# Two outlook-attention layers: layer 1's weights reach their source row in the table transfer, not in 0/1 matmuls

## The chip, the cores and the metric

The kernel runs on one core of one Trainium2 chip, in float32. The metric is the device time of one launch in microseconds (us). Three runs of the kernel before took 3530.87, 3531.84 and 3535.32 us; the median is 3531.84 us. The profile is one further execution, which took 3516.74 us.

## The reference, cut to what matters

The input is 8 images of 56 x 56 pixels with 384 channels. Two layers follow each other, each a group normalisation, a convolution-like attention and a residual. Layer 1 is:

```python
a = jax.nn.softmax((x @ W_attn + b_attn).reshape(B, H * W, heads, k * k), axis=-1)   # heads 6, k 3
v = x @ W_v + b_v
vp = jnp.pad(v, ((0, 0), (1, 1), (1, 1), (0, 0)))
patches = stack([vp[:, i:i + H, j:j + W] for i in range(k) for j in range(k)])
y = einsum('bpKhd,bphK->bphd', patches, a)          # nine weighted neighbours per pixel and head
return y @ W_proj + b_proj
```

Each pixel weighs its 3 x 3 neighbours. Seen from a neighbour (the source), its weight belongs to a pixel one row above, on the same row, or one row below. The kernel wants the weights ordered by source row, so each weight with row offset `ki` has to move by `ki - 1` rows; weights whose source lies outside the image must not count. Layer 0 is of the same kind with nine softmaxes per head and a fold.

## The kernel before, in words

**Tiling.** Two images are laid over each other (`R = 112` rows) and one image column of both is one step. Columns are taken in patches of `PX = 7`; a patch of an image pair is a *group*, numbered g, and there are `NG = 32` groups. Layer 1's main loop (`for step in range((NG + 1) * PX)`, L1016) runs seven steps m = 0 to 6 per group. In layer 1 nearly every operation goes through a wrapper that keeps the order in which the code is written (`InOrder`, L124; its instructions all show as L132, matmuls as L119, transposes as L122). So the order on each engine is the order of the loop. Layer 0's vector and scalar operations are ordered by the framework's scheduler.

**What a step does.** `attend` (L843) multiplies 128 normalised tokens by the joint weights for logits and values (tile `bank`), and VectorE adds the biases into `lgt` and `v`. When the column number is a multiple of 8, `attend` does nothing. GpSimd's queue writes `v` to the value table `vtab1` (`spread`, L311).

**What a group does, in the steps that follow its own.** `keep_logits` (L867) writes the logits to DRAM at m = 0 (`lgtab`), `read_logits` (L879) reads them back with image rows on the partitions (tile `at`, m = 1), `weigh` (L893, m = 3) and `share` (L901, m = 4) make the softmax on VectorE with one exp on ScalarE, and `move` (L909, m = 5) does this:

- three matmuls with the constant 0/1 matrices `shift` (L168), one per row offset `ki`, give `pw` in PSUM, the weights of source row r. Out-of-image weights are zeroed by the matrices. TensorE carries each as two instructions.
- nine ScalarE copies bring `pw` into `wz`, each 112 x 42, so that the seven pixels of the patch lie one element apart in neighbouring slots (the band).
- one transfer from ScalarE's queue writes `wz` to a weight table in DRAM (`ztab1`, three of them in turn): 112 rows x 9 slots, one piece of 3 x 42 floats (504 bytes) each.

At m = 0 of the next group `fetch` (L938) issues from SyncE's queue, in this order: four reads of the table as band matrices (`z`), two reads of the values (`vp`), then, at m = 1, the load of the residual (`x1t`, `load`, L797) and the read of the logits (`at`). From m = 3 on, the contraction `pc`, the output projection `po` and the transposes `pt` of that group are taken from a list of jobs (`Jobs`, L339), two per step.

**The tables' zeros.** What no transfer of weights writes is zeroed once, in layer 0: `clear_weights` (L215) issues four transfers from SyncE for each of the three tables of layer 0 (steps 5, 14, 21) and of layer 1 (steps 35, 42, 49). `inside` (L182) holds for each row offset and row a 1, or a 0 where the neighbour is outside.

**Instructions per engine around the change.** At m = 5, ScalarE's order is: two copies `yT<-pc`, the nine `wz` copies, the table transfer, `ot` (a transposed output), two copies `yT<-pc`, the normalisation `xn` of the next patch. TensorE's order is: 48 `pc` matmuls, the six `pw` instructions, `bank`, a transpose, 36 `pc`, `bank`, a transpose, and then `po`, which needs every `yT`.

Of the kernel before, what the change touches and what calls it, by code (L numbers as in the profile page):

```python
# [8 lines left out]
F32 = mybir.dt.float32  # L9
AF = mybir.ActivationFunctionType  # L10
# [5 lines left out]
def two_outlook_layers(  # L16
# [38 lines left out]
    R = IMG * H  # L55
    MARGIN = 2
# [8 lines left out]
    PX = 7  # L65
# [4 lines left out]
    HEADS0, HEADS1 = 12, 6  # L70
    D0, D1 = C // HEADS0, C // HEADS1
    K, K2 = 3, 9
# [12 lines left out]
    PY1, NPY1, SX1, SY1 = 8, 7, PX + 2, 10  # L85
    ROW1 = HEADS1 * PX
# [8 lines left out]
    EP1, FIRST1 = 11, 4  # L95
    SLOT0, SLOT1 = EP0 * ROW0, EP1 * ROW1
    LINE0, LINE1 = SX0 * SLOT0 + ROW0, SX1 * SLOT1 + ROW1
# [20 lines left out]
    def matmul(*args, **kwargs):  # L118
        tc.keep_in_program_order(nc.tensor.matmul(*args, **kwargs))  # L119
# [48 lines left out]
    shift = const.tile([R, K, R], F32, name="shift")  # L168
    gpsimd.memset(shift, 0.0)
    for k in range(-1, 2):  # L170
        s = shift[:, k + 1, :]
# [10 lines left out]
    inside = const.tile([R, K, PH_ALL], F32, name="inside")  # L182
# [12 lines left out]
    def fill(table, first, dims, width):  # L195

        src = zeros[: dims[0][1], :width]
        if len(dims) > 1:
            src = src.unsqueeze(1).to_broadcast([dims[0][1], dims[1][1], width])
        tc.keep_in_program_order(  # L200
            nc.sync.dma_start(bass.AP(table.tensor, table.offset + first, [*dims, [1, width]]), src)
        )
# [12 lines left out]
    def clear_weights(table, line, part, sx, slot, row, first, e, ep):  # L215
        fill(table, 0, [[part, MARGIN * line // part]], part)
        fill(table, (MARGIN + R) * line, [[part, (MARGIN + 1) * line // part]], part)
        top = MARGIN * line
        fill(table, top, [[line, R]], first * row)
        fill(table, top + (first + e) * row, [[line, R], [slot, sx]], (ep - e) * row)  # L220

    def clears():

        yield 3, lambda: clear_v(vtab0, SX0, 2)

        yield 4, lambda: fill(
            ztab0[0], MARGIN * LINE0 + FIRST0 * ROW0, [[LINE0, R], [SLOT0, 2]], E0 * ROW0
        )
        for n, t in enumerate(ztab0):
            yield (5, 2 * PX, 3 * PX)[n], lambda t=t: clear_weights(  # L230
                t, LINE0, 366, SX0, SLOT0, ROW0, FIRST0, E0, EP0
            )
        yield 4 * PX, lambda: clear_v(vtab1, SX1, 1)
        for n, t in enumerate(ztab1):
            yield (5 + n) * PX, lambda t=t: clear_weights(
                t, LINE1, 350, SX1, SLOT1, ROW1, FIRST1, K, EP1
            )
# [116 lines left out]
    ps = ctx.enter_context(tc.tile_pool(name="ps", bufs=1, space=PS))  # L354
# [429 lines left out]
    def layer1(pools, base, last_of_layer0, late_w):  # L784
        vector, scalar, sync = (InOrder(e) for e in (nc.vector, nc.scalar, nc.sync))
# [53 lines left out]
        NW = SX1 * K * ROW1  # L839
# [68 lines left out]

        def move(g):  # L909

            at = lgs.pop(g)

            pw = ps.tile([R, K, PX, K, HEADS1], F32, tag="f", name=f"pw1_{g}")
            for ki in range(K):
                matmul(
                    pw[:, K - 1 - ki].rearrange("r x f h -> r x (f h)"),
                    shift[:, ki, :],
                    at.rearrange("r x (i j) h -> r x i (j h)", j=K)[:, :, ki, :],
                    start=True, stop=True,
                )  # L920

            wz = wzs[g % 2]
            step = K * ROW1 + 1
            for kj in range(K):
                dst = wz[:, kj * K * ROW1 : kj * K * ROW1 + PX * step].rearrange("r (m e) -> r m e", e=step)
                dst = dst[:, :, : K * ROW1].rearrange("r m (e h o) -> r e m h o", e=K, h=HEADS1)
                for e in range(K):
                    scalar.copy(dst[:, e, :, :, 0], pw[:, e, :, kj, :])
            table = ztab1[g % NTAB]
            scalar.dma_start(  # L930
                bass.AP(
                    table.tensor, table.offset + MARGIN * LINE1 + FIRST1 * ROW1,
                    [[LINE1, R], [SLOT1, SX1], [1, K * ROW1]],
                ),
                wz[:, :NW].rearrange("r (s e) -> r s e", s=SX1),
            )

        def fetch(g, due):  # L938
            pair, px = divmod(g, NPX)
# [76 lines left out]
        for step in range((NG + 1) * PX):  # L1016
            g, m = divmod(step, PX)
# [3 lines left out]
            read, first, second, moved = (0, 2, 3, 4) if last else (1, 3, 4, 5)  # L1021
# [10 lines left out]
            if g and m == moved:  # L1032
                move(done)
# [69 lines left out]
```

## Time and profile before

| | us |
|---|---|
| median of three runs (3530.87 to 3535.32) | 3531.84 |
| the profiled execution: its time / its span | 3516.74 / 3514.6 |
| TensorE busy in the span | 3427.7 (98%) |
| ScalarE, VectorE, GpSimd busy | 1173.3, 1935.8, 1202.1 |
| layer 1's `pw` matmuls: 192 instructions, mean 290 ns each | 29.7 in the instruction's own time |
| `wz` copies: 288, mean 269 ns | 31.8 |
| table writes `ztab<-wz`: 32 of 496.1 KB, issue to landing | 4.4 |

How to read it: the span runs from the first to the last instruction; the time of the execution has a little around it. Matmuls overlap each other in the array, so the sum of their own times is more than the time they take from the engine; the distance from start to start tells that. A transfer has two times: how long its issue holds the queue, and how long it takes from issue to landing. Layer 1 begins at about 2320 us; its groups follow each other from about 2390 to 3440 us.

### The profile page before, as it was taken

The numbers are of one execution on the slowest core, as the hardware profiler recorded it, in microseconds if no ns is written. First come the engines' busy times: TensorE is split into PE (matmuls) and PEld (weight loads), VectorE is DVE, ScalarE is ACT, GpSimd is POOL, SyncE is SP. The second block draws the span as 40 slices with busy tenths as digits, with TensorE's granted clock in tenths as the row PEclk, the third lists the DMA queues.
The fourth block names the chain that finished last, engine by engine and source line by source line (L and its number), as shares of the span: only waits on it lengthen the run. The fifth ranks groups of instructions, "written<-read, shape, count | busy, mean of one in ns | idle before, by whom it ended". The sixth has DMA issues, their size and how long they took to land. (4 is left out here: it accounts for less than half of the span.)

```text
span 3514.6 us, 72311 instructions
## 1 busy us (share of the span) xinstructions
PE 3427.7 (98%) x29014; PEld 2353.0 (67%) x29014; DVE 1935.8 (55%) x4680; ACT 1173.3 (33%) x2727; POOL 1202.1 (34%) x1833
## 2 busy tenths in 40 slices
PE   7899999999999999999999999988999999999998
PEld 5577777777777777777777777655666666666665
DVE  6666666667666676667766666633333333333331
ACT  4333223333333233333322223223434434343432
POOL 2543434434344344344443444331222222221220
PEclk8999999999999999999999999999999999999998
DMA  8999988688886878887757776676878787878775
GB/s 270 286 288 282 275 275 267 212 256 253 279 263 209 272 221 273 259 252 256 236 181 226 245 225 193 222 271 192 226 221 234 217 229 219 243 205 237 216 219 147
DMA packets 672893, 839.34 MB, mean 239 GB/s; under 512 B 302190, under 2 KB 566574, under 8 KB 668462
## 3 DMA queue, kind: packets, MB, share of 16 engines
q1 hardware_dynamic: 321422, 537.46, 47.9%
q10 hardware_dynamic: 323872, 210.54, 22.7%
q0 software_dynamic: 27264, 86.73, 7.5%
q8 instruction: 228, 3.74, 0.5%
q14 instruction: 107, 0.88, 0.1%
HBM read 512.95 MB, written 321.66 MB: 237 GB/s over the span
## 5 line engine op out<-in xcount | busy, mean ns | idle before, releaser
L119 PE MATMUL bank<-wa_t,xn 128*112 128x288 f32 x4032 | 1086.9, 409 | 11.4 <-ACT v L562 7.8
L574 POOL TENSOR_TENSOR at<-at,den 112x972 f32<-112x972 f32 x224 | 504.6, 2253 | 1193.1 <-DVE den L573 1137.8
L119 PEld LDWEIGHTS bank<-wa_t,xn 128*112 128x112 f32 x4032 | 693.4, 177 | 263.7 <-issue 34.3
L119 PE MATMUL po<-yT,wo_t 128*128 128x448 f32 (+1 forms) x2304 | 817.5, 494 | 5.3 <-DVE x1t L685 4.8
L119 PEld LDWEIGHTS po<-yT,wo_t 128*128 128x128 f32 x2304 | 432.8, 191 | 293.5 <-issue 185.4
L119 PE MATMUL pc<-z,vp 121*32 121x49 f32 (+1 forms) x17664 | 487.9, 254 | 25.3 <-DMA vp<-vtab 10.4
L119 PEld LDWEIGHTS pc<-z,vp 121*32 121x32 f32 (+1 forms) x17664 | 441.3, 131 | 103.3 <-issue 79.5
L550 DVE TENSOR_REDUCE mx<-bank 112x36 f32<-112x324 f32 x672 | 327.6, 487 | 310.6 <-PE bank L119 303.7
L317 POOL DMA_DIRECT2D vtab<-v x392 | 213.1, 547 | 825.3 <-DVE v L132 810.4
L119 PE MATMUL bank<-wc_t,xn 128*128 128x438 f32 x1176 | 478.8, 543 | 5.0 <-DMA wo_t<-in_wo 5.0
L119 PE MATMUL bank<-wv_t,xn 128*128 128x384 f32 x1176 | 417.9, 492 | 0.0
L555 ACT ACTIVATE at<-at 112x972 f32<-112x972 f32 x224 | 227.0, 1014 | 344.9 <-DVE at L551 317.6
L551 DVE TENSOR_TENSOR at<-bank,mx 112x324 f32<-112x324 f32 x672 | 328.8, 489 | 21.1 <-DVE mx L550 0.5
L119 PEld LDWEIGHTS bank<-wc_t,xn 128*128 128x128 f32 x1176 | 214.0, 191 | 174.8 <-issue 162.4
L119 PEld LDWEIGHTS bank<-wv_t,xn 128*128 128x128 f32 x1176 | 219.5, 190 | 139.6 <-issue 18.7
L619 ACT COPY wt<-pw 112x120 f32<-112x120 f32 x224 | 58.0, 259 | 654.0 <-PE pw L119 591.2
L597 POOL TENSOR_TENSOR pre<-at,at 112x108 f32<-112x108 f32 (+1 forms) x440 | 238.0, 541 | 110.4 <-DVE wt L620 96.0
L567 DVE TENSOR_TENSOR d<-at 112x432 f32<-112x432 f32 x224 | 141.7, 632 | 204.7 <-ACT at L555 204.7
L132 DVE TENSOR_TENSOR lgt<-bank,ba_t 128x54 f32<-128x54 f32 x196 | 41.7, 213 | 361.3 <-PE bank L119 361.3
L132 DVE SCALAR_TENSOR_TENSOR x1t<-po,bo_t,x1t 128x448 f32<-128x448 f32 (+1 forms) x156 | 97.7, 626 | 248.9 <-PE po L119 248.9
L664 ACT COPY yT<-pc 128x294 f32<-128x294 f32 x256 | 103.4, 407 | 368.9 <-PE pc L119 325.9
L535 ACT ACTIVATE xn<-xin,bias,scale 128x224 f32<-128x224 f32 x336 | 172.9, 566 | 67.2 <-PE bank L119 36.0
(100 smaller groups left out, 2924.6 us busy)
## 6 DMA issues: line engine op xcount, KB each, us to landing
z<-ztab SPq DMA_DIRECT2D x64, 2352.0 KB, 18.0
vp<-vtab SPq DMA_DIRECT2D x64, 1536.0 KB, 8.3
ztab<-wt ACTq DMA_DIRECT2D x336, 183.8 KB, 6.8
vp<-vtab SPq DMA_DIRECT2D x64, 945.0 KB, 12.0
xres<-xT SPq DMA_DIRECT2D x32, 1176.0 KB, 10.1
xin<-xT ACTq DMA_DIRECT2D x54, 672.0 KB, 7.3
z<-ztab SPq DMA_DIRECT2D x128, 258.4 KB, 4.5
x1t<-x SPq DMA_DIRECT2D x26, 1176.0 KB, 19.0
```

The lines of the kernel that those rows point to most:

```text
L119: tc.keep_in_program_order(nc.tensor.matmul(*args, **kwargs))
L132: return lambda *args, **kwargs: tc.keep_in_program_order(op(*args, **kwargs))
L317: queue.dma_start(bass.AP(table.tensor, table.offset + first, [[line, rows], [(R + GAP) * line - PX * C, n], [1, C]],), v.unsqueeze(1).to_ ...
L535: nc.scalar.activation(to[:, i, :, rows], xin[:, i, :, rows], AF.Identity, bias=bias[:, i, b : b + 1], scale=scale[:, i, b : b + 1],)
L550: nc.vector.tensor_reduce(mx[:, pi, :], pl.rearrange("r q a -> r a q"), AX.X, ALU.max)
L551: nc.vector.tensor_tensor(at[:, pi], pl, mx[:, pi, :].unsqueeze(1).to_broadcast([R, K2, PH]), ALU.subtract)
L555: nc.scalar.activation(at, at, AF.Exp, scale=SCALE0)
L567: nc.vector.tensor_add(d4, at[:, :, 0:4], at[:, :, 4:8])
L574: nc.gpsimd.tensor_tensor(at, at, den.unsqueeze(2).to_broadcast([R, K, K2, PH]), ALU.mult)
L597: nc.gpsimd.tensor_tensor(dst, terms[0], terms[1], ALU.add)
L619: nc.scalar.copy(mid[:, 0 : E0 : E0 - 1, :], pw[:, 0 : E0 : E0 - 1, :])
L664: nc.scalar.copy(yT[:, :, :, b, rows_of], pc.rearrange("p i n y m -> p i m (n y)"))
```

## The change

In layer 1 the weights stay on the partition of the pixel they belong to, and the transfer into the table writes them to the source's row. The nine copies become nine activations (`Copy` with a scale) that read the softmax result `at` in SBUF; the scale is the 0 or 1 of `inside` for the two outer row offsets, and the constant 1.0 for the middle one. The single transfer becomes three, one per row offset e, each to the row above, the same row, or the row below, with pieces of 42 floats (168 bytes). `clear_weights`, which layer 0 uses too, zeroes two more strips of each table: the places in the first and last row that no weight is moved to. The three matmuls and the PSUM tile `pw` of layer 1 are gone; layer 0 still uses `shift`.

```diff
@@ clear_weights @@
+        fill(table, top + first * row, [[slot, sx]], row)
+        fill(table, top + (R - 1) * line + (first + e - 1) * row, [[slot, sx]], row)
@@ move @@
-            pw = ps.tile([R, K, PX, K, HEADS1], F32, tag="f", name=f"pw1_{g}")
-            for ki in range(K):
-                matmul(
-                    pw[:, K - 1 - ki].rearrange("r x f h -> r x (f h)"),
-                    shift[:, ki, :],
-                    at.rearrange("r x (i j) h -> r x i (j h)", j=K)[:, :, ki, :],
-                    start=True, stop=True,
-                )
+            at = at.rearrange("r x (i j) h -> r i x j h", j=K)
...
-                for e in range(K):
-                    scalar.copy(dst[:, e, :, :, 0], pw[:, e, :, kj, :])
+                for ki in range(K):
+                    scalar.activation(
+                        dst[:, K - 1 - ki, :, :, 0], at[:, ki, :, kj, :], AF.Copy,
+                        scale=inside[:, ki, 0:1] if ki != 1 else 1.0,
+                    )
             table = ztab1[g % NTAB]
-            scalar.dma_start(
-                bass.AP(
-                    table.tensor, table.offset + MARGIN * LINE1 + FIRST1 * ROW1,
-                    [[LINE1, R], [SLOT1, SX1], [1, K * ROW1]],
-                ),
-                wz[:, :NW].rearrange("r (s e) -> r s e", s=SX1),
-            )
+            for e in range(K):
+                scalar.dma_start(
+                    bass.AP(
+                        table.tensor,
+                        table.offset + (MARGIN + 1 - e) * LINE1 + (FIRST1 + e) * ROW1,
+                        [[LINE1, R], [SLOT1, SX1], [1, ROW1]],
+                    ),
+                    wz[:, :NW].rearrange("r (s e w) -> r e s w", s=SX1, e=K)[:, e],
+                )
```

In the built programs the order on TensorE, VectorE and GpSimd in layer 1 is otherwise the same; ScalarE's differs by the lines above. In layer 0 the scheduler orders some operations of steps 5 to 12 differently.

## Prediction

> **What bounds the kernel now.** I read the page's first two parts for the whole, then the stage in which the change lies: one window over the steady groups of layer 1, two stretches of the timeline, the waits of SyncE's queue, and the DMA queues in short windows.
>
> ```profile
> PE 3427.7 (98%) x29014; PEld 2353.0 (67%) x29014; DVE 1935.8 (55%) x4680; ACT 1173.3 (33%) x2727; POOL 1202.1 (34%) x1833
> ...
> DMA  8999988688886878887757776676878787878775
> ```
>
> ```profile
> 2427.00:3397.00 970.00, 968.48 (x7496) 606.67 (x7495) 307.59 (x652) 389.83 (x1143) 216.37 (x399) 1.00 0.80 225
> ```
>
> The second fence is layer 1 from the table write of group 2 (2427.09) to that of group 30 (3397.11): TensorE is busy 968 of 970 us, so it sets the pace, 970.0 / 28 = 34.64 us per group. But the last columns say that the DMA engines are busy 80% of the same time. That calls for a second look: is there a chain of transfers that is nearly as long as the pace?
>
> ```profile
> 2911.77 0.31 ACTq L132 DMA_DIRECT2D ztab<-wz  x1
> ...
> 2916.18 1.79 SPq L132 DMA_DIRECT2D z<-ztab  x4
> ...
> 2918.26 0.86 SPq L132 DMA_DIRECT2D vp<-vtab  x2
> ...
> 2919.23 4.25 SPq L132 DMA_DIRECT2D x1t<-x  x1
> ...
> 2939.05 0.84 DVE L132 TENSOR_REDUCE mx<-at 112x42 f32<-112x378 f32 x1 [4.35 <-DMA at<-lgtab]
> ...
> 2942.39 0.55 DVE L132 TENSOR_TENSOR at<-at,den 112x378 f32<-112x378 f32 x1
> ...
> 2944.09 0.91 PE L119 MATMUL pw<-at,shift 112*112 112x126 f32 x6
> ...
> 2944.84 2.37 PE L119 MATMUL bank<-wc_t,xn 128*128 128x438 f32 x6
> 2945.03 0.99 ACT L132 COPY wz<-pw 112x42 f32<-112x42 f32 x9 [0.39 <-PE pw L119]
> 2946.06 0.31 ACTq L132 DMA_DIRECT2D ztab<-wz  x1
> ```
>
> ```profile
> SPq L132 <- DMA ztab<-wz: 546.1, 31, 25.4
> ```
>
> There is, and it is a **loop**. SyncE's queue holds the `z` reads until the table write has landed (31 waits); `vp`, `x1t` and the next logits (`at`) stand behind them in the same queue; VectorE's `mx` waits for `at`; the softmax ends in `at<-at,den`; then come `pw`, `wz` and the next table write. Over 28 groups the means from one write's issue are: `z` issued at 4.27, `mx` starts at 27.60, softmax done at 31.50, and 1.97 from the start of `pw` to the next issue: 33.47 us. TensorE's 34.64 is longer by only 1.2 us.
>
> ```profile
> q10 hardware_dynamic: 721, 0.36, 91.9%
> ...
> q1 hardware_dynamic: 2535, 3.76, 80.5%
> q0 software_dynamic: 373, 1.27, 19.3%
> q10 hardware_dynamic: 912, 0.19, 6.2%
> ...
> q1 hardware_dynamic: 675, 0.14, 95.9%
> ...
> q10 hardware_dynamic: 424, 0.09, 91.2%
> ```
>
> Queues in windows (packets, MB, share of 16 engines). The first line is the table write alone (2844.5 to 2846). The next three (2918 to 2936, from just behind the `z` issue to near the landing of `at`) add up to 106%: there the engines are full, so what starts later ends later by as much. The last two are small packets: the logits' read (2937.5 to 2938.2) and their write (3163.5 to 3164), 216 bytes each.
>
> **What the Trainium skill says.** "DMA: Bandwidth & Descriptors", section "Issuing engines are not separate DMA queues": transfers of all queues share the same 16 engines. The 106% agrees. Same page, "Why small descriptors are slow (HBM only)": each packet carries a fixed overhead beside its bytes, so a third of the bytes costs more than a third of the time. The trace agrees: 721 packets of 504 bytes took 1.5 us x 16 x 0.919 / 721 = 30.6 ns each; those of 216 bytes 0.7 x 16 x 0.959 / 675 = 15.9 (read) and 0.5 x 16 x 0.912 / 424 = 17.2 (write). "ScalarE: Activation LUTs", section "What ACT_TABLE_LOAD costs": an operand per partition, such as the new scale, adds about 93 ns to an ACTIVATE. No run here isolates that.
>
> **The change part by part.**
>
> *Matmuls removed.* From `pw` to the next matmul is 0.75 us (2944.09 to 2944.84): 32 x 0.75 = 24.0 us if nothing else is late. In the groups where `attend` is left out at m = 5 or 6 (8 of 32), `po` comes 2.2 us sooner behind `pc` and meets ScalarE's copies; there I count 0.1 to 0.3. Mean 0.61, so TensorE alone would give 34.03 us per group.
>
> *Nine activations for nine copies.* The copies take 1.03 us up to the issue. By that page's price (186 + 0.833 x 42 ns, 93 more with the scale, 93 of it under the next) a 42-element ACTIVATE advances by 0.22 us with the scale and 0.13 without: 6 x 0.22 + 3 x 0.13 + 0.14 for the end = 1.85, an estimate. Bounds: 1.03 (they run like the copies) and 3.0 (each like the `xn` of 168 elements, which follow each other by 0.42, less 0.10 for 126 elements). I take 1.85. They no longer wait for `pw` (0.39 wait), so softmax-to-issue is 0.05 + 1.85 = 1.90 instead of 1.97.
>
> *Three transfers for one.* Two more issues hold ScalarE 0.36 each; 0.31 is the measured issue. What is queued behind: `ot`, two `yT`, `xn`; `po` and the next `bank` wait for those. Counting from the end of the 48 `pc`, ScalarE may begin `wz` up to 2.2 us later before `po` waits (`po` at 7.2 - 0.75; ScalarE needs 1.85 + 1.0 + 0.5 + 0.7 ahead of it); now it begins at about 0.6. So this is hidden as long as the softmax is on time. Packets: 3 x (1008 + 16) = 3072 instead of 1024. Before: 1024 x 30.6 / 16 = 1.96 us. After: between 14.2 ns (the line through 216 and 504 bytes, drawn on to 168) and 30.6 ns (a flat price per packet); no row shows 168 bytes. I take 16, near the measured 216: 3.07 us, 1.1 more; and 0.2 for the value writes it now overlaps. So the `z` issue comes **1.3 us later** (0.8 to 3.9), and with full engines behind it, so does `at`.
>
> *The loop then:* 31.50 + 1.3 + 1.90 = 34.70 us, against 34.03 that TensorE wants and 34.64 now. The loop sets the pace: 30 groups x 0.06 = **+2 us**. The 24 us are not lost on TensorE, they become its waiting.
>
> *The `vp` reads* move with `z`: they land about 12 us after issue, some 20 us after the 48 `pc`; first needed at 24.7, now 24.0. With 1.3 later that leaves 2.
>
> *Clears.* Twelve tiny transfers on SyncE. Those for layer 1's tables wait for nothing late. Those for layer 0 overlap strips that the folds of the same table write, so a fold's write on ScalarE's queue waits for them, once per table; the first stand behind a 2.4 MB clear. Behind the wait on ScalarE stand copies that free PSUM banks. 0 to 10 us in all, below nothing where the reordering helps (-2). I take **+3**.
>
> *Tail.* The last group's write goes 0.3 sooner and lands 1.3 later, the reads behind it with some 3 us to spare before their `pc` (3482.09): nothing.
>
> Sum: +5 us. The profiled execution (3516.74, span 3514.6) becomes 3522; it lies 15.1 below the median of the runs, whose figure becomes 3531.84 + 5 = 3537.
>
> **The rivals.** *The matmuls' time arrives.* If the read of the logits ends when it did, because the work moved in the queues fills the idle stretch behind `mx`, TensorE keeps the pace: 30 x -0.61 + 3 = -15, 3517. For it: TensorE is at 99.8% now, and the DMA engines are idle in part of every group. Against: the 106%, and the softmax only 1.2 us early. *Price per packet flat (ends slower).* 3072 x 30.6 / 16 = 5.9 us, 3.9 more: loop 37.3, 30 x 2.7 + 3 = +83, 3615. It decides from the point where the extra landing passes 1.25 us. Against: the 216-byte rows. *ScalarE held by the clears in layer 0* for more than 10 us, with the loop as forecast: 3550. That the change doesn't do what it says: the program has no layer-1 `pw`; excluded.
>
> **How the numbers follow.** Loop at 0.8 to 2.0 us more landing: chance 0.58, own range 3521 to 3558, time 3537; of it 0.13 faster, 0.24 same, 0.21 slower. Matmul time arrives: 0.27 (0.25 faster, 0.02 same). Flat price, or something between: 0.10, slower. Clears: 0.05, slower. Faster 0.38, same 0.26, slower 0.36, counted beyond 0.2% (7 us), about what a measurement of this kernel can tell from no change. Range 3514 to 3573: below is less than the removed matmuls allow, above are landings of over 2.5 us more.
>
> **What would show it.** Right: `z` issued 5.2 to 6 us behind the first table issue; `mx` to next issue shorter or equal; `wz` waiting for VectorE's `at`; TensorE with new waits for `yT` and `xn`, its busy time some 20 us down with the span unchanged; the period near 34.7. Wrong: no new TensorE waits and a period of 34.0 (first rival), or `z` 8 us behind (second), or layer 0 ending later than 2315 us by over 5 us (third).

## The result, and the profile after

| | before | after |
|---|---|---|
| median of the runs | 3531.86 us (3530.87 to 3535.32) | 3743.68 us (3740.34 to 3747.57) |
| span of the profiled execution | 3514.6 us | 3738.6 us |

The changed kernel is **slower: 1.0596 times before, 95% interval 1.0580 to 1.0612**, 211.8 us. Read the page first, its busy times and its slices:

```profile
PE 3497.7 (94%) x28822; PEld 2390.5 (64%) x28822; DVE 1935.3 (52%) x4680; ACT 1192.3 (32%) x2727; POOL 1201.5 (32%) x1833
...
PEclk8999999999999999999999999988999999999997
DMA  8999987798887688877577676787898888888886
```

TensorE has 192 matmuls fewer and yet 70 us more of busy time, at a lower share; the DMA share in the last third is up. Next, the window over the same 28 groups of layer 1, from the first table write of group 2 (2452.1) to that of group 30 (3602.06):

```profile
2452.00:3602.00 1150.00, 1028.40 (x7325) 637.99 (x7325) 306.54 (x652) 407.24 (x1143) 216.39 (x399) 0.92 0.87 190
```

The period is 1150.0 / 28 = **41.07 us** instead of 34.64. TensorE no longer sets it: it is idle for 122 of 1150 us, and at a granted clock of 0.92 instead of 1.00. Then one group of it, on the timeline:

```profile
2907.45 2.17 ACTq L132 DMA_DIRECT2D ztab<-wz  x3
...
2917.27 1.94 SPq L132 DMA_DIRECT2D z<-ztab  x4
2919.51 1.80 SPq L132 DMA_DIRECT2D vp<-vtab  x2
2921.42 2.86 SPq L132 DMA_DIRECT2D x1t<-x  x1
...
2924.55 0.31 SPq L132 DMA_DIRECT2D at<-lgtab  x1
...
2941.59 0.83 DVE L132 TENSOR_REDUCE mx<-at 112x42 f32<-112x378 f32 x1 [9.02 <-DMA at<-lgtab]
...
2944.32 1.61 PE L119 MATMUL pc<-z,vp 90*64 90x56 f32 x48 [3.06 <-ACT yT L132]
...
2944.90 0.55 DVE L132 TENSOR_TENSOR at<-at,den 112x378 f32<-112x378 f32 x1
...
2945.97 0.44 ACT L132 COPY yT<-pc 128x336 f32<-128x336 f32 x1 [0.26 <-PE pc L119]
2946.31 0.38 ACT L132 ACTIVATE wz<-at,inside 112x42 f32<-112x42 f32 x1
...
2948.20 1.70 ACTq L132 DMA_DIRECT2D ztab<-wz  x3
```

It is the loop of the prediction, and `z` is issued 9.82 us behind the first table issue; the forecast was 5.2 to 6. Means over the 28 groups, from the timelines of both kernels:

| part of the loop (us) | before | after | difference |
|---|---|---|---|
| first table issue to `z` issue | 4.27 | 10.46 | +6.19 |
| `z` issue to the start of `mx` | 23.33 | 23.43 | +0.10 |
| `mx` to the end of the softmax | 3.90 | 3.87 | -0.03 |
| softmax to the next table issue | 3.14 | 3.31 | +0.17 |
| period | 34.64 | 41.07 | +6.43 |

So nearly all of the longer period is the landing of the table write. One wait in this loop the prediction left out: before SyncE can issue the read `at`, the logits' write `lgtab` must have landed. For this the queue stands still in the kernel before, over its 28 groups (2427 to 3397):

```profile
SPq L132 <- DMA lgtab<-lgt: 272.0, 27, 13.8
...
DVE mx L132 <- DMA at<-lgtab: 104.5, 28, 5.6
```

In the changed kernel it does so for 9.3 us in all, because `z` comes later in the same queue. That `z` to `mx` takes 23.3 to 23.5 us in both kernels and in one_transfer, although these waits differ, is measured; why isn't settled.

Over the whole execution: layer 1's first table write comes 18.8 us later (2412.74 for 2393.98), the 31 steps to its last one take 196.2 more, and the tail behind it 9.1 more: 224.0 with rounding, the difference of the two spans. The waits say who pays, SyncE's queue in the first line, the rest in the same window:

```profile
SPq L132 <- DMA ztab<-wz: 897.8, 28, 34.7
```

```profile
DVE mx L132 <- DMA at<-lgtab: 279.3, 28, 13.3
...
PEld pc L119 <- ACT yT L132: 78.1, 30, 6.8
...
PE pc L119 <- ACT yT L132: 70.2, 24, 6.6
...
PE pc L119 <- DMA vp<-vtab: 47.1, 18, 5.3
```

VectorE waits 10 us per group for the logits (3.7 before: 104.5 / 28); TensorE, through `yT` copies that stand behind the late exponential on ScalarE, and through `vp`, waits for the same thing. In the kernel before its waits for `yT` in this stretch are 1.5 us (`PE`), and it has none for `vp`.

### The profile page after: what moved, and what is told of

The parts are those of the page before. It is cut to its first block, busy times and chain, and to the rows that moved or that the text cites. A ratio compares the mean times of both kernels' runs of the same rounds, so it can differ in the third digit from the quotient of the medians.

```text
span 3738.6 us, 71995 instructions
## 1 busy us (share of the span) xinstructions
PE 3497.7 (94%) x28822; PEld 2390.5 (64%) x28822; DVE 1935.3 (52%) x4680; ACT 1192.3 (32%) x2727; POOL 1201.5 (32%) x1833
## 4 chain that ended last, share of the span: by engine, by line
PE 70%; DMA 20%; issue 4%; ACT 2%; DVE 2%; SPq 1%; ACTq 1%; POOL 0%; POOLq 0%; DVEq 0%
PE bank L119 40%; PE po L119 13%; PE pc L119 10%; DMA at<-lgtab 9%; PE pw L119 3%; DMA vp<-vtab 3%; DMA ztab<-wz 2%; PE pt L122 1%; DMA ztab<-zeros 1%; DMA lgtab<-lgt 1%; SPq L132 1%; ACT xn L132 1%; DMA xr<-in_x 1%; DMA xres<-xT 1%; DMA vtab<-v 1%
## 5 line engine op out<-in xcount | busy, mean ns | idle before, releaser
L119 PE MATMUL pc<-z,vp 121*32 121x49 f32 (+1 forms) x17664 | 522.7, 261 | 172.9 <-ACT yT L132 76.7
L119 PEld LDWEIGHTS pc<-z,vp 121*32 121x32 f32 (+1 forms) x17664 | 475.1, 138 | 254.4 <-issue 99.6
L119 PE MATMUL bank<-wc_t,xn 128*128 128x438 f32 x1176 | 525.7, 587 | 5.5 <-ACT xn L132 5.5
L119 PEld LDWEIGHTS bank<-wc_t,xn 128*128 128x128 f32 x1176 | 232.6, 208 | 199.5 <-issue 181.5
```

## The experiments

Figures in the table are means over 28 groups of layer 1 (timeline and packet records). "Last packet" counts from the first table issue to the end of the last packet of the write that carries weights; "held" are packets of the write in a group that took over 100 ns. "Parts" is worked out from the access patterns: how many of a group's piece ends (two each, the beginning and the end) do not fall on a multiple of 32 bytes in the table, if the table itself begins on one; the text calls them ragged ends. A ratio is to the kernel before on the same chip. The runs stand on several chips: middle_only, gaps, aligned and logits_first share one, start64 and half_block another, one_wz_first, clears_layer1 and padded a third. With the same three writes `z` came at 9.45 (clears_layer1), 10.46 (after) and 10.95 (after_again), so small differences between chips mean little. In middle_only, gaps, aligned, start64, half_block and the one_ runs a part of the computation is left out.

| run | ratio (95% interval) | period | `z` at | last packet | held | parts |
|---|---|---|---|---|---|---|
| before | 1 | 34.64 | 4.27 | 3.49 | 0 | 1456 |
| after | 1.0596 (1.0580 to 1.0612) | 41.07 | 10.46 | 7.41 | 122 | 4592 |
| after_again | 1.0627 (1.0606 to 1.0647) | 41.75 | 10.95 | 7.81 | 133 | 4592 |
| one_transfer | 1.0049 (1.0036 to 1.0062) | 35.00 | 4.35 | 3.50 | 0 | 1456 |
| three_pieces | 1.0498 (1.0484 to 1.0513) | 40.57 | 9.28 | 6.40 | 85 | 4592 |
| three_issues | 1.0007 (0.9998 to 1.0016) | 34.86 | 4.53 | 3.62 | 1 | 1456 |
| middle_only | 1.0038 (1.0027 to 1.0048) | 35.23 | 4.22 | 2.57 | 0 | 1568 |
| gaps | 1.0500 (1.0484 to 1.0517) | 40.17 | 9.04 | 6.35 | 78 | 4480 |
| start64 | 1.0288 (1.0255 to 1.0321) | 38.21 | 7.00 | 5.16 | 2 | 3024 |
| half_block | 1.0209 (1.0179 to 1.0239) | 37.27 | 6.27 | 5.35 | 0 | 0 |
| aligned | 1.0227 (1.0208 to 1.0245) | 37.09 | 6.07 | 5.30 | 0 | 0 |
| logits_first | 1.0264 (1.0248 to 1.0280) | 37.35 | 9.52 | 6.87 | 76 | 4592 |
| one_wz_first | 1.0016 (1.0007 to 1.0025) | 34.93 | 4.81 | 3.85 | 0 | 1456 |
| one_logits_first | 0.9946 (0.9930 to 0.9962) | 33.93 | 4.69 | 3.39 | 0 | 1456 |
| clears_alone | 1.0024 (1.0017 to 1.0031) | 34.74 | 4.43 | 3.62 | 0 | 1456 |
| clears_layer1 | 1.0492 (1.0475 to 1.0508) | 40.69 | 9.45 | 6.43 | 86 | 4592 |
| padded | 1.0058 (1.0044 to 1.0073) | 35.10 | 5.44 | 4.55 | 0 | 0 |
| padded_sync_behind | 1.0037 (1.0020 to 1.0054) | 34.93 | 6.13 | 5.27 | 0 | 0 |
| padded_sync | 0.9981 (0.9972 to 0.9990) | 34.12 | 5.88 | 5.01 | 0 | 0 |

### Is it the three writes?

One write in the changed kernel:

```diff
-            for e in range(K):
-                scalar.dma_start(
...
-                        table.offset + (MARGIN + 1 - e) * LINE1 + (FIRST1 + e) * ROW1,
-                        [[LINE1, R], [SLOT1, SX1], [1, ROW1]],
...
+            scalar.dma_start(
...
+                    table.tensor, table.offset + MARGIN * LINE1 + FIRST1 * ROW1,
+                    [[LINE1, R], [SLOT1, SX1], [1, K * ROW1]],
```

> The changed kernel, with its three table writes put back to one of 504-byte pieces, so the rows are not moved (that part of layer 1's computation is left out). Theory (the three writes cost it all in layer 1): z is issued about 4.3 us behind the write as before, the period of a group falls from 41.1 to 34.0 to 34.7 us, and only layer 0's loss of some 18 us is left: 3520 to 3550 us. Rival (nine activations with a scale, on ScalarE ahead of the write, hold the loop): z at 4.3, but softmax to issue longer, period above 36, over 3590 us.

The write costs nothing more once it is one of 504 bytes. But the period was 35.00, above the 34.0 to 34.7 that were expected: the matmuls are gone and no time is won. That is taken up below. In the kernel before, the reverse, three writes at the rows where they were, first by pieces of a slot (three_pieces, 3 x 1008 pieces of 168 bytes), then by slots (three_issues, 3 x 336 pieces of 504 bytes):

```diff
-                    table.tensor, table.offset + MARGIN * LINE1 + FIRST1 * ROW1,
-                    [[LINE1, R], [SLOT1, SX1], [1, K * ROW1]],
+            for e in range(K):
...
+                        table.tensor, table.offset + MARGIN * LINE1 + (FIRST1 + e) * ROW1,
+                        [[LINE1, R], [SLOT1, SX1], [1, ROW1]],
```

```diff
-                    table.tensor, table.offset + MARGIN * LINE1 + FIRST1 * ROW1,
-                    [[LINE1, R], [SLOT1, SX1], [1, K * ROW1]],
+            for s in range(0, SX1, K):
...
+                        table.tensor, table.offset + MARGIN * LINE1 + FIRST1 * ROW1 + s * SLOT1,
+                        [[LINE1, R], [SLOT1, K], [1, K * ROW1]],
```

> The kernel before, its 0/1 matmuls kept, with its one table write split into three of 168-byte pieces at the rows where they were. Theory (pieces): z issued about 10 us behind the first issue, period 40 to 41.5 us, 3700 to 3740 us. Rival (the cost needs the row above or below, or the activations): period below 36, under 3570 us.

> The kernel before, with its table write split into three transfers of three slots each, pieces of 504 bytes as before. Theory (number and size of the pieces): 1008 pieces as before, z some 0.5 to 1.5 us later than 4.3 by the two further issues, period 34.6 to 35.7, 3530 to 3565 us. Rival (the number of issues and semaphores): z at 8 to 10 us, period about 40, about 3700 us.

Both side with the theory of pieces, with somewhat lower figures than it gave: three_pieces took 3693 us and three_issues 3521, below their ranges, where before took 3518. Three issues alone put `z` at 4.53, one on the same chip at 4.43 (clears_alone); three times as many pieces put it 5 us later, without any activation or move of rows. The 1.2 us from there to the changed kernel's 10.46 are within what chips differ by.

### What is it in the pieces?

The packets of the write, in the four us from its issue and the four after (packets, MB, share of 16 engines), in the changed kernel (2907.45):

```profile
q10 hardware_dynamic: 2393, 0.40, 70.2%
...
q10 hardware_dynamic: 679, 0.11, 60.7%
```

The first 2393 took 4 x 16 x 0.702 / 2393 = 18.8 ns each, the last 679 took 57 ns each, so a price per packet is not what binds: they begin cheaply and are then held. The median stays 15 ns. And `z` is issued 3.05 us after the end of the last packet of weights (before: 0.78), so the write isn't over when these are out. Five edits to the pieces of the changed kernel, in the order middle_only, gaps, aligned, start64, half_block; in the last three SLOT1 is 464 and LINE1 4208, so the steps from slot to slot and from row to row change too. Not shown: the tables' clears and, in the last three, the source pattern are adapted.

```diff
-            for e in range(K):
+            for e in (1,):
...
-                        table.offset + (MARGIN + 1 - e) * LINE1 + (FIRST1 + e) * ROW1,
-                        [[LINE1, R], [SLOT1, SX1], [1, ROW1]],
...
+                        table.offset + (MARGIN + 1 - e) * LINE1 + (FIRST1 + 2 * e) * ROW1,
...
+                        table.offset + (MARGIN + 1 - e) * LINE1 + 160 + 48 * e,
+                        [[LINE1, R], [SLOT1, SX1], [1, 48]],
...
+                        table.offset + (MARGIN + 1 - e) * LINE1 + 160 + 48 * e,
+                        [[LINE1, R], [SLOT1, SX1], [1, 42]],
...
+                        table.offset + (MARGIN + 1 - e) * LINE1 + 168 + 48 * e,
+                        [[LINE1, R], [SLOT1, SX1], [1, 48]],
```

> The changed kernel with only the middle one of its three table writes: 1008 pieces of 168 bytes to the pixel's own row (the pieces for the rows above and below are left out of the computation). Theory (the writes pile up: the first 1008 go in at 15 ns each, later ones are held): z about 3.0 to 3.8 us behind the issue, earlier than with one write of 504 bytes (4.3), and the time at or a little below that of the run with one 504-byte write, 1.000 to 1.005 of before. Rival (a write of such pieces completes late by itself, some 3 us after its last packet): z at 6 us or later, 1.01 to 1.03 of before.

A miss at the edge: `z` at 4.22, not 3.0 to 3.8. The packets are out at 2.57 and none was held, but `z` is issued 1.65 behind them, twice the 0.78 of before.

> The changed kernel with the three pieces of a slot set one row width (168 bytes) apart, so that no two pieces of different writes touch each other (the reads then take wrong columns: the order of the weights is left out of the computation). Theory A (number of pieces): unchanged, z at 9.5 to 11 us, 1.055 to 1.065 of before. Theory B (neighbouring pieces, written from different rows at nearly the same time, hold each other up): z falls to 5 to 7 us, 1.00 to 1.025 of before.

Theory B falls: pieces that don't touch are held as much (three_pieces 9.28, gaps 9.04). Theory A's range (9.5 to 11, 1.055 or more) is missed too, from below.

> The changed kernel with pieces of 192 bytes that begin at multiples of 64 bytes in the table (slots of 1856 and rows of 16832 bytes; the columns read are then not those written, which leaves the weights' places out of the computation), the number of pieces unchanged. Theory B2 (a piece that covers blocks of memory in part is what costs): z falls to 5 to 7 us, 1.00 to 1.025 of before. Theory A (number of pieces below some size): z at 9.5 to 12 us, 1.055 to 1.07.

Here B2 holds and A falls: as many pieces, a seventh more bytes, and none is held. The same two stretches as above:

```profile
q10 hardware_dynamic: 2858, 0.54, 72.5%
...
q10 hardware_dynamic: 214, 0.04, 4.9%
```

16.2 ns a packet (4 x 16 x 0.725 / 2858), and `z` 0.77 behind the last. That is the figure of the prediction, 16. The two that vary where the pieces begin and end, with the slots and rows of aligned:

> As aligned (pieces begin at multiples of 64 bytes), but 168 bytes long again, so that only the start of a piece is on a block and its end is not (the columns read are not those written, which leaves the weights' places out). Theory S (where a piece begins decides): z at 5.5 to 6.5 us, no packets held over 100 ns. Theory E (every block covered in part costs, at the end as at the start): half of the partial blocks are left, z at 7 to 9 us, some packets held.

> As aligned (pieces of 192 bytes), but begun 32 bytes past a multiple of 64 (again with the weights' places left out). Theory 64 (the block is 64 bytes): two partial blocks for each piece as in the changed kernel, z at 8.5 to 11 us, over 80 packets held beyond 100 ns in a group. Theory 32 (the block is 32 bytes): whole blocks, z at 5.5 to 6.5 us, none held.

Theory E, at the lower edge of its range (7.00, with 2 packets held), and theory 32. On one chip and with the same slots and rows, a start 32 bytes past a multiple of 64 does no harm (6.27), and one ragged end per piece puts `z` 0.73 us later (7.00) though an eighth fewer bytes are written. Among the runs with 3024 pieces the column "parts" goes with the landing: 0 gives 5.4 to 6.3, 3024 gives 7.0, 4480 to 4592 give 9.0 to 11.0. A count by blocks of 16 bytes would give start64, gaps and the changed kernel 3024 each, and one by 64 would give half_block 6048; neither goes with the landing.

The figures per part, as estimates: 0.73 us / 3024 = 0.24 ns for the first 3024, then (9.04 - 7.00) / 1456 = 1.4 ns to (10.46 - 7.00) / 1568 = 2.2 ns. The second step is weaker evidence than the first. It goes from one chip to another and also changes the step from slot to slot (1848 for 1856 bytes) and from row to row (16800 for 16832). A run with the slots and rows of aligned and both ends ragged is missing, so a share of the changed steps in these 2 to 3.5 us isn't excluded; padded, further down, has other steps again (2112 and 19200 bytes), no ragged end, and none held. With 1456 parts and packets of 504 bytes, the write before shows no arrears. What happens to a block that is covered in part isn't shown. The Trainium skill, "DMA: Bandwidth & Descriptors", section "Specifications", puts a limit at 512 bytes, below which a transfer does read-modify-write. Here pieces of 192 bytes were not held when they covered whole blocks, so in this case it isn't the size alone that decides.

### Why do the matmuls' 0.6 us not arrive?

With one write (one_transfer) TensorE is busy 959.42 of 980 us, and the rest is waits for `yT`:

```profile
2438.00:3418.00 980.00, 959.42 (x7325) 594.00 (x7325) 307.20 (x652) 409.73 (x1142) 216.38 (x399) 0.99 0.80 223
```

```profile
PEld pc L119 <- ACT yT L132: 25.6, 22, 3.5
PE pc L119 <- ACT yT L132: 20.3, 15, 3.3
```

Two readings: the loop of transfers is the pace, or the nine activations are, since `yT` copies stand behind them. First the order on ScalarE, `move(done)` ahead of the step's first `jobs.run`:

```diff
+            if g and m == moved:
+                move(done)
             jobs.run(base + step, 1)
...
-            if g and m == moved:
-                move(done)
```

> The run with one 504-byte write (rows not moved, which leaves that part of the computation out), with the nine activations and the write issued ahead of the contraction of the same step instead of behind it. Theory (the wz activations stand behind two yT copies in ScalarE's order, and those wait for 48 pc that a late exponential has put off): softmax to issue falls from 3.3 to about 2.0 us, the period from 35.0 to 34.0 to 34.3, where TensorE is the pace: 0.994 to 0.999 of before. Rival (the nine activations by themselves hold TensorE): period 34.8 or more, 1.003 to 1.006.

A miss for the theory; the rival has the period but not the ratio (1.0016). Softmax to issue fell from 3.29 to 2.40, but the softmax itself ended 0.8 us later (32.53 for 31.71), 0.46 of it as `z` was later; the period hardly moved (34.93). This did not tell the readings apart. The next does: the logits' read ahead of the `x1t` load, which shortens the loop and leaves the activations.

```diff
-            if m == 1 and g + 1 < NG:
-                load(g + 1)
...
             if g and m == read:
                 read_logits(done)
+            if m == 1 and g + 1 < NG:
+                load(g + 1)
```

> The run with one 504-byte write (rows not moved, which leaves that part of the computation out), and the logits' read ahead of the x1t load. Theory (the loop of transfers keeps the matmuls' time from arriving, even with the write as before): the logits land 2 to 4 us sooner, the period falls from 35.0 to 34.0 to 34.3, TensorE's waits for yT go: 0.994 to 0.999 of before. Rival (the nine activations, longer than the copies, hold the yT copies on ScalarE and so TensorE): softmax is sooner but the period stays at 34.8 or more, 1.003 to 1.006.

```profile
2455.00:3406.00 951.00, 951.00 (x7331) 589.00 (x7329) 308.90 (x654) 414.07 (x1145) 216.37 (x399) 1.00 0.82 229
```

```profile
PEld pc L119 <- ACT yT L132: 0.7, 4, 0.2
```

It was the loop. `mx` starts at 25.20 instead of 27.83, TensorE is busy all the time again, and its own pace is 33.93 us. In the changed kernel the same edit gives back part:

> The changed kernel with the read of the logits issued ahead of the x1t load on SyncE's queue, nothing else. Theory (the loop of transfers sets the pace, and x1t's 1176 KB stand in it): at lands some 4 to 6 us sooner, the period falls from 41 to 35 to 37 us, 1.01 to 1.03 of before. Rival (the engines' share decides, or x1t becomes what is late): period 39 or more, over 1.045.

37.35 instead of 41 us, above the range, though its ratio is in it: `z` is at 9.52 still.

### The clears

> The kernel before with the two further clears per table and nothing else. Theory (the clears delay the first table writes of layer 0 behind them): layer 0 ends 10 to 20 us later, 3542 to 3552 us. Rival (layer 0's loss in the changed kernel has another cause, such as the granted clock): 3528 to 3536 us.

Some 8.5 us (0.24% of 3518), less than the 10 to 20 expected though not nothing; the time itself, 3528.4 us, lies in the rival's range only because before took 3518 on this chip. Some of ScalarE's waits in the first 600 us of that run, of a kind that the kernel before does not show there:

```profile
ACT yT L667 <- DMA ztab<-zeros: 9.3, 1, 9.3
...
ACT at L558 <- DMA ztab<-zeros: 7.2, 1, 7.2
...
ACT wt L622 <- DMA ztab<-wt: 4.5, 1, 4.5
```

In the first two ScalarE stands until clears of a table have landed: a copy (`yT`, at 415 us) and an exponential (at 274 us) are behind a table write of layer 0 in its queue. The waits can't be summed to a loss: the kernel before stands once for 12.5 us, at 154 us, where this run doesn't. Clears for layer 1's tables alone (`if sx == SX1:` ahead of the two fills):

> The changed kernel with the further clears made for layer 1's three tables alone, none for layer 0's. Theory (the clears of layer 0's tables stop ScalarE's queue three times in the first 480 us): the waits of ScalarE for the tables' clears go, layer 0 ends as in the kernel before, the period of layer 1 stays at 41: 1.053 to 1.057 of before. Rival (layer 0's loss has another cause): layer 0 still 9 us or more late, 1.059 to 1.061.

One such wait is left, 9.9 us, of the three (29.0 us) that the changed kernel has. It is the one at 416 us, 10 us behind the further clears of layer 1's first table (406 us). It stands in clears_alone, padded and the changed kernel too, and in none of before, three_pieces and three_issues, which lack these clears; so the prediction's "Those for layer 1's tables wait for nothing late" doesn't hold. Nor does layer 1 begin as before: its first table write comes at 2401.1 us, as it does with all clears on the same chip (one_wz_first, 2401.1). The ratio, below the range expected, fell by more than the clears explain. That is partly the chip: the changed kernel once more, elsewhere, is this:

> The changed kernel itself once more, on the chip of these runs, so that its parts can be set against it there: 1.050 to 1.062 of before.

1.0627, just above what was expected, so its ratio moves with the chip and the two numbers can't be subtracted.

### A version that uses this

Entries of 48 floats instead of 42 in table, `wz` and `z` (two `z` buffers and four `v` buffers, to make room, and every fifth `x1t` load in two parts), the logits first, `wz` first, clears for layer 1 alone:

> The whole computation, with the four findings together: table entries padded to 192 bytes (pieces at multiples of 64 bytes, two z buffers instead of three and four v buffers instead of five to make room), the logits' read ahead of the x1t load, wz ahead of the contraction, and the clears for layer 1 alone. Theory (loop = z issue + transfers up to the logits + softmax + wz): z at about 6, logits some 3 us sooner, loop 33.0 to 34.0, so TensorE sets the pace at 34.0 to 34.5 again: 0.994 to 1.000 of before. Rival (another wait is next: z buffers, x1t, or reads grown by a seventh): period over 35, 1.01 or more.

It misses its range, and the wait is not one that the rival named: ScalarE stands still while it issues the three writes, and TensorE waits for the copies behind them (first two lines ScalarE, third TensorE):

```profile
2537.13 2.31 ACTq L132 DMA_DIRECT2D ztab<-wz  x3
2539.48 0.78 ACT L132 COPY yT<-pc 128x336 f32<-128x336 f32 x2 [2.38 <-issue]
...
2539.97 1.75 PE L119 MATMUL pc<-z,vp 90*64 90x56 f32 x36 [3.18 <-ACT yT L132]
```

So `sync.dma_start` for the three, on the queue in which `z` is next:

> As padded (whole computation), but with the three table writes issued from SyncE's queue, where z comes next anyway, and wz behind the contraction's yT copies as in the changed kernel. Theory (ScalarE is held 2.3 to 2.7 us by the three issues, and the next yT copies with it): TensorE's waits of up to 3.2 us for yT go, period 33.7 to 34.4, 0.990 to 0.999 of before. Rival (the loop is too long with wz behind): period over 34.8, 1.003 or more.

> As the run before it, with wz ahead of the contraction as in padded. Theory: loop about 33, TensorE alone sets the pace, 33.5 to 34.1 per group: 0.988 to 0.997 of before. Rival (wz ahead of the yT copies delays those by 1.9 us and TensorE with them): slower than with wz behind, 34.1 or more.

```profile
2437.00:3392.00 955.00, 951.45 (x7350) 589.41 (x7346) 308.84 (x652) 406.11 (x1142) 217.17 (x401) 1.00 0.88 235
```

With `wz` behind the contraction the loop is too long (34.93, the rival); with `wz` ahead TensorE is busy 951 of 955 us, and the whole computation takes **0.9981 (0.9972 to 0.9990)** of before, a gain that is just measurable and a little short of the forecast. Here the order on ScalarE does matter: 34.93 against 34.12. The groups win more than that, 34.64 - 34.12 = 0.52 us each, about 15 us in all (an estimate). Part of it is lost at the end: from the last table write to the end of the span it is 64.5 us instead of 52.9, with one wait of 10.8 us of a `pc` for `z`. No run goes into that.

## Why the prediction was wrong

The forecast was 3537 us, range to 3573. The mechanism was right; two terms of its sum were mis-sized, and the first of them by enough to break the range.

- **The loop of transfers takes over from TensorE, and the matmuls' time becomes waiting.** Right; one_transfer and one_logits_first show it, the latter with 33.93 us for TensorE alone (34.03 forecast).
- **"I take 16, near the measured 216: 3.07 us, 1.1 more" and so "z issue comes 1.3 us later (0.8 to 3.9)".** This is the step that failed. 16 ns is what a packet costs when it isn't held (15 median, 16.2 aligned), and the aligned pieces put `z` at 6.07, not far above the 5.6 forecast. The landing came 6.19 us later, above the upper bound, because both bounds were prices per packet. This write is limited by something else, which three_pieces shows to lie in the pieces and which goes with their ragged ends; the write before, with a third as many, does not show it. This is 4.9 of the 6.4 us by which the loop is longer than forecast.
- **"softmax-to-issue is 0.05 + 1.85 = 1.90 instead of 1.97".** Failed too: 3.31 (3.29 in one_transfer). The 1.97 counted from `pw`; from the softmax the kernel before needs 3.14. I took the 1.17 between as waiting for TensorE's pace that would go. It stays: `wz` begins as the `yT` copy ahead of it on ScalarE ends, and that copy needs 48 `pc` which TensorE began late (2944.32 above, a wait of 3.06 for an earlier `yT` copy behind the exponential). This is 1.4 of the 6.4 us. With `wz` moved ahead of that copy 0.9 of it went, but the softmax came as much later (one_wz_first), so the place in ScalarE's order alone isn't all of it. Even one write gave 35.0, not 34.0; the first rival (3517) was out of reach.
- **Nine activations in 1.85 us.** Right: 2946.31 to 2948.20, 1.89. One with the scale is followed after 0.23 us, one without after 0.13, the 93 ns that the prediction took from the Trainium skill ("ScalarE: Activation LUTs", section "What ACT_TABLE_LOAD costs").
- **Two issues at 0.36 each.** Low: the three hold ScalarE 2.17 us in the group shown, and in the mean the first takes 0.31, the second 0.65 and the third 0.91; why they grow isn't shown. It is this that padded_sync takes from ScalarE: it differs from padded in the queue alone, and the period falls from 35.10 to 34.12.
- **The `vp` reads "leaves 2".** Not contradicted: with 6 us instead of 1.3 the margin is gone, 47.1 us of waits in 28 groups.
- **Clears +3.** 8.5 alone (6.0 to 10.9). Layer 1's first table write comes 18.8 us later in the profiles; the part beyond the clears, some 10 us, isn't settled. Single executions differ by more than that: with the same clears this write comes at 2397.9 us in clears_alone and at 2422.3 in one_logits_first, on one chip. The third rival's sign came as well: layer 0's last table write is at 2330.6 instead of 2312.6. The granted clock of the first two stretches of 120 us was lower (0.84 and 0.94 against 0.86 and 0.97), and I can't say whether as cause or effect.
- **Tail: nothing.** It is 9.1 us: `z` of the last group comes 10.77 us behind its write instead of 3.85, and the last `pc` wait for `vp`.
- **The rival "price per packet flat"** had the side and the place right and gave 3615, but not the cause: the packets that aren't held cost 15 to 16 ns, not 30.6. Its sign, `z` 8 us behind, came. Even it was 129 us short.

## What to carry to other kernels

Before a write is cut into smaller pieces, count two things, its packets and the ends of its pieces that fall inside a 32-byte block; here the trace of the larger pieces priced the first and showed nothing of the second. Padding the entries to whole blocks bought 3 to 4 us of landing per group (gaps to aligned 9.04 to 6.07; clears_layer1 to padded 9.45 to 5.44, with other edits). When two cycles are within a few per cent of each other (34.6 and 33.5), measure the second from the same point to the same point in program order, with every in-order engine that it passes, before a gain on the first is booked.

## What the runs showed that was not expected

- The end of the packets that carry weights isn't the end of a write: `z` follows the last of them by 0.77 to 0.91 us when all blocks are whole (aligned, half_block), by 1.84 with 3024 partial ones (start64), by 3.05 with 4592. With 1008 pieces it is 1.65 for 1568 partial blocks (middle_only) but 0.78 for the 1456 of the larger, slower packets of before.
- In this kernel TensorE loses twice by a wait: in the changed kernel it is idle 4.3 us per group, but the period is 7.1 above its own pace of 33.9. The rest is busy time, 36.7 us a group instead of 34.0, at a granted clock of 0.92. The six `bank` matmuls at 2908.04 took 4.46 us at a clock of 0.50 (2908.04 to 2912), those at 2914.92 took 2.37 at 1.00. From 2400 to 3660 us the clock is at 0.5 in 31 stretches, 205 us together, and each of them lies within 10 us behind a TensorE wait of over 1.5 us.
